# A graph layer on one core: source blocks of 732 instead of 640, overflow edges fetched inside the loop, and 128 edge ranges instead of 120

## The chip, the core and the metric

The kernel runs on one core of a Trainium2 chip. A core has TensorE (PE: matmuls, with PEld for its weight loads), VectorE (DVE), ScalarE (ACT), GpSimd (POOL), SyncE (SP, which here only issues transfers) and 16 DMA engines that all transfers share. Each engine runs its own list of instructions in order; they meet through semaphores. The metric is the device time of one execution in microseconds (us). Three runs of the kernel before took 16521.81, 16530.51 and 16532.21 us; the median is 16530.51.

## The reference

100,000 nodes have 64 features each. There are 3,300,000 edges (src, dst), sorted by dst: 1.6 million random pairs in both directions and one self-loop per node.

```
h = relu(layernorm(x))
y[e] = concat(h[dst], h[src] - h[dst]) @ W.T + b      for each edge e
s = segment_sum(y, dst);  cnt = segment_sum(1, dst)
out = x + where(cnt > 0, s / max(cnt, 1), 0)
```

The layer is linear in h[src], so what costs time is the sum of h[src] over the edges of each dst; the two products with W follow once per node.

## The kernel before, in words

**Table.** A first stage computes h and writes it to DRAM as `h3`: for each node 194 bf16 values, that is h cut into three bf16 parts (3 x 64), a one for the count and one value of padding, 388 bytes. Matmuls use the first 193 columns.

**Two ways to sum edges.** The edges are split by position. The last part goes through `chunks` (L344): 3584 edges at a time; POOL gathers the rows h3[src] with 28 indirect DMAs of 128 rows each (L388), DVE builds a one-hot matrix of dst (`one_hot`, L336 to L342), PE multiplies it with the rows, 28 matmuls of 193 columns (L393), and POOL adds the sums to `acc` in DRAM (L365 or L370). The first part is cut into `NW` = 120 *ranges* of 16,256 edges, which go through `pairs` (L743) two at a time (60 *sets*). Both ways share all engines, and the amounts of each are constants: `U0` sets and `PA` chunks come before a loop, and each of the loop's three iterations does `SB` sets and `KB` chunks.

**Sorting the ranges.** `sort_windows` (L415) sorts each range by source, one range per partition, all 120 at once: each merge step is a copy on ACT (L449) and a min and a max on DVE (L450, L451). It yields a nominal cost in ns after each step, and the main program then issues one chunk gather for every `GATHER` ns (1230) of it. At step 40 and at every second step after it, one block of `h3` is copied to `tables` in DRAM (L891, on SP); `tables` holds per partition what a block load needs in one run. Nothing ties these copies to the sort, so the scheduler that orders the instruction lists may move them forward.

**Slots.** A source block is `CS` = 640 nodes, in two halves of 320. In every sorted range, each half of a block gets `KS` = 64 slots. `fill_slots` (L681) fetches the keys of the slots by indirect DMA, 12 for each group of six blocks (L692), and DVE and ACT turn them into source numbers (`sr_d`) and dst numbers (`dt_d`). Edges of a half beyond its 64 slots, up to `SPILL` = 128 per range, are found by `find_beyond` (L634): 128 scans on DVE (L641), 120 indirect DMAs for their keys (L663), and two small tables `xs_d` and `xt_d` in DRAM.

**A set in `pairs`.** It steps through `NE` = 162 items: `NCB` = 157 blocks, four items of self-loops, and one item of overflow edges. `fetch` (8 items ahead) has SP load tables (three blocks per load, three buffers, L764), `srs` and `dt` (six blocks per load), the rows of the set's own nodes, and `xs` and `xt`; POOL gathers the overflow rows (L782). `one_hots` (two items per instruction) compares on DVE: `gh` picks a source within three sub-blocks of 128 (L796), `dh` places it among 512 dst nodes (L339). `pick` multiplies: three matmuls of 193 columns for each range and block (L822), then two copies on ACT (L825, L826). `put` adds into PSUM: eight matmuls for each item (L836). With halves of 320 nodes, sub-blocks 0 to 2 serve one half and 2 to 4 the other, so the middle one is shared and a `limit` test (L706, L707) keeps the halves apart.

The first `U0` = 3 sets start while `fill_slots` still runs: from its fourth group on, three steps (six items) of `pairs` follow each group. The remaining steps of these sets, with chunk gathers between, follow after it, then the rest of the `PA` = 71 chunks, then the loop.

Sizes that follow from the constants:

```
              sets  before loop / per iteration   chunks before / per iteration   items   blocks
before          60        3 / 19                        71 / 102                   162     157
after           64        1 / 21                        59 / 94                    144     137
```

Of the kernel before, what the change touches and what calls it, by code (L numbers as in the profile page):

```python
# [13 lines left out]
F32 = mybir.dt.float32  # L14
BF16 = mybir.dt.bfloat16
# [9 lines left out]
DVE = mybir.EngineType.DVE  # L25

# [4 lines left out]
SB = 19  # L31
KB = 102
U0 = 3
KG = 16
JH = 14
LAG = 3
GATHER = 1230
# [5 lines left out]
CS = 640  # L43
NB = CS // P
KH = P // 2
# [3 lines left out]
SPILL = 128  # L49
# [39 lines left out]
FIRST = 71  # L89
# [3 lines left out]
def gnn_preln(ctx: ExitStack, tc, x, src_w, dst_w, src_p, dst_p, src_a, dst_a, wT, b, out, V, E):  # L93
# [32 lines left out]
    NE = NS + 1  # L126
# [3 lines left out]
    RT = max(R, NCB * CS)  # L130
# [5 lines left out]
    assert NT == 4 and NB == 5 and CSH == 2 * P + KH  # L136
    assert 2 * C == P and NS % 2 == 1 and NW <= P and PA >= 0
# [13 lines left out]
    xs_d = dram.tile([SPILL, NW], I32, name="xs_d")  # L151
    xt_d = dram.tile([SPILL, NW, NH * D], I16, name="xt_d")
    tables = dram.tile([NTB, P, TG, NB * CT], BF16, name="tables")
# [157 lines left out]
    with tc.tile_pool(name="rows", bufs=5) as rows, \  # L311
# [103 lines left out]
        def sort_windows(keys, piece, small, ps):  # L415
# [32 lines left out]
            def exchange(lo, hi, tmp):  # L448
                nc.scalar.copy(tmp, lo)  # L449
                nc.vector.tensor_tensor(lo, tmp, hi, ALU.min)  # L450
                last[DVE] = nc.vector.tensor_tensor(hi, tmp, hi, ALU.max)  # L451
# [160 lines left out]
            nc.gpsimd.iota(first, pattern=[[CS, NS], [CSH - KH, 2]], base=BIAS >> 10, channel_multiplier=0)  # L612
            turned = piece.tile([NW, 2], F32, name="turned", bufs=1)
            nc.vector.tensor_scalar(turned, par, float(CSH - KH), None, op0=ALU.mult)
# [3 lines left out]
            limit = small.tile([NW, 2], F32, name="limit", bufs=1)  # L618
            nc.vector.tensor_scalar(limit[:, 0:1], par[:, 0:1], float(KH), float(CSH), op0=ALU.mult, op1=ALU.add)
            nc.vector.tensor_scalar(limit[:, 1:2], par[:, 0:1], float(-KH), float(CSH + KH), op0=ALU.mult, op1=ALU.add)  # L620
# [10 lines left out]
            slots[:] = at_i, first, row, fit, over, limit  # L631
            last.pop(DVE)

        def find_beyond(piece):  # L634

            row, fit, over = slots[2:5]
# [8 lines left out]
            nc.vector.tensor_scalar(xno, iota[:NW, :SPILL], over[:, NHB - 1:], None, op0=ALU.is_ge)  # L645
            nc.vector.tensor_add(xpos, xpos, iota[:NW, :SPILL])
# [5 lines left out]
            b_ps = g_ps.tile([P, 512], F32, name="gp")  # L652
            b_ps = b_ps[:, :2 * NW].rearrange("p (i w) -> p i w", i=2)
            for i in range(2):
                nc.tensor.transpose(b_ps[:, i], beyond[:, i], ident[:NW, :NW])
            xat = piece.tile([P, NW], I32, name="xat", bufs=1)
            nc.vector.tensor_copy(xat, b_ps[:, 0])
            xno = piece.tile([P, NW], F32, name="xno", bufs=1)
            nc.vector.tensor_copy(xno, b_ps[:, 1])
            yield  # L660
            kx = piece.tile([P, NW], I32, name="kx", bufs=1)
            for w in range(NW):
                last[POOL] = nc.gpsimd.indirect_dma_start(  # L663
                    out=kx[:, w:w + 1], out_offset=None, in_=ksort,
                    in_offset=bass.IndirectOffsetOnAxis(ap=xat[:, w:w + 1], axis=0))
                if w % 8 == 7:
                    yield
            xs = piece.tile([P, NW], I32, name="xs", bufs=1)
            nc.vector.tensor_scalar(xs, kx, 10, None, op0=ALU.logical_shift_right)
            nc.vector.tensor_scalar(xs, xs, float(-(BIAS >> 10)), float(V), op0=ALU.add, op1=ALU.min)  # L670
            nc.sync.dma_start(xs_d, xs)
            nc.vector.tensor_scalar(kx, kx, 1, CH - 1, op0=ALU.logical_shift_right, op1=ALU.bitwise_and)
            rx = piece.tile([P, NW], F32, name="rx", bufs=1)
            nc.vector.scalar_tensor_tensor(rx, xno, float(2 * CH), kx, op0=ALU.mult, op1=ALU.add)
            xt = piece.tile([P, NW, NH, D], I16, name="xt", bufs=1)
            for half in range(NH):
                nc.vector.tensor_scalar(xt[:, :, half], rx[:, :, None].to_broadcast([P, NW, D]), float(-half * HALF), None,
                                        op0=ALU.add)
            nc.sync.dma_start(xt_d.rearrange("s w i -> s (w i)"), xt.rearrange("s w h d -> s (w h d)"))

        def fill_slots(piece):  # L681
            at_i, first, limit = *slots[:2], slots[5]
# [3 lines left out]
            for c0 in range(0, NS, SL):  # L686
# [13 lines left out]

                df = piece.tile([NW, SL, P], F32, name="df", bufs=1)
                past = df.bitcast(I32).rearrange("w c (q s) -> w (c q) s", q=2)[:, :2 * mb]
                if mb:
                    for q in range(2):
                        of = [a.rearrange("w (c q) s -> w c q s", q=2)[:, :, q] for a in (past, sr[:, :2 * mb])]
                        nc.vector.tensor_scalar(*of, limit[:, q:q + 1], float(2 * CS), op0=ALU.is_ge, op1=ALU.mult)  # L706
                    nc.vector.tensor_tensor(sr[:, :2 * mb], sr[:, :2 * mb], past, ALU.add)  # L707
# [35 lines left out]
        def pairs(base, n, late=None):  # L743
# [4 lines left out]
            def fetch(t):  # L748
# [12 lines left out]
                if s < NCB and s % TG == 0:  # L761
                    m = min(TG, NCB - s)
                    tabs[u, s // TG] = tab = load.tile([P, TG, NB, CT], BF16, name="tab")
                    nc.sync.dma_start(tab[:, :m].rearrange("p c b f -> p (c b f)"),  # L764
                                      tables[s // TG][:, :m].rearrange("p c x -> p (c x)"))
# [5 lines left out]
                if s == (late if late and u == 0 else NE // 4):  # L771
                    at = ds((base + u) * 2, 2)
                    xs = load.tile([P, 2], I32, name="xs", bufs=2)
                    nc.sync.dma_start(xs, xs_d[:, at])
                    xt = load.tile([P, 2 * NH, D], I16, name="xt", bufs=2)
                    nc.sync.dma_start(xt.rearrange("p i d -> p (i d)"), xt_d[:, at].rearrange("s w i -> s (w i)"))
                    rows_x = load.tile([P, 2, CT], BF16, name="rows_x", bufs=2)
                    beyond[u] = xs, xt, rows_x
                if s == (NE - 2 if late and u == 0 else NE // 3):
                    xs, xt, rows_x = beyond[u]  # L780
                    for i in range(2):
                        last[POOL] = nc.gpsimd.indirect_dma_start(  # L782
                            out=rows_x[:, i], out_offset=None, in_=h3,
                            in_offset=bass.IndirectOffsetOnAxis(ap=xs[:, i:i + 1], axis=0))

            def one_hots(t):
                u, s = divmod(t, NE)
                if u < n:
                    m = min(2, NS - s)
# [3 lines left out]
                    for a, z, to in ((0, mb, NT - 1), (mb, m, NT)):  # L793
                        if a < z:
# [6 lines left out]
                    one_hot(dh[:, :m].rearrange("p c i (h n) -> p (c i h) n", h=NH),  # L801
                            dts[u, s // SL][:, c:c + m].rearrange("p c i d -> p (c i) d"), HALF)
                    if m < 2:
                        one_hot(dh[:, 1].rearrange("p i (h n) -> p (i h) n", h=NH), beyond[u][1], HALF)
# [248 lines left out]
```

## Time and profile before

| what | value |
|---|---|
| median of three runs | 16530.51 us |
| the profiled execution's own time | 16529.2 us |
| its span, first to last instruction | 16527.4 us |
| PE busy | 13495.8 us (82%) |
| DVE busy | 13631.9 us (82%) |
| POOL busy | 11625.4 us (70%) |
| ACT busy | 10590.2 us (64%) |
| DMA, mean over the span | 240 GB/s |
| loop, three iterations | about 3995 to 16203 us |

The page gives for each engine its busy time, then the span in 40 slices, where a digit is the busy share in tenths. PEclk is the granted TensorE clock, also in tenths. A group line names source line, engine, operation, output and inputs, then busy time, mean ns of one, and the idle time ahead of it with what ended it. "issue" marks idle time in which the engine waited for nothing that the profile shows. A busy share over the whole span mixes stages with different limits, so stages are read in windows of time.

### The profile page before, as it was taken

The page shows a single profiled execution, that of the slowest core. Times are in us where ns is not written, and L with a number is a line of the kernel's source. Part 1 is how long each engine was busy: PE and PEld are TensorE (multiplying, and loading weights), DVE is VectorE, ACT ScalarE, POOL GpSimd, SP SyncE. Part 2 cuts the span into 40 slices and gives each one's busy share as a digit, 9 for nine tenths or more (in the row PEclk, how much of TensorE's full clock was granted, in tenths as well). Part 3 has the DMA queues.
Part 4 walks back from the last instruction along what each step waited for, and adds up shares of the span by engine and source line. Part 5 has one row for each costly group of instructions (what it writes and reads, how often), then busy time and mean ns, then how long its engine had stood idle before and what let it go on. Part 6 is the DMA issues. An engine that isn't in the chain of part 4 may idle for free. (4 is left out here: it accounts for less than half of the span.)

```text
span 16527.4 us, 393944 instructions
## 1 busy us (share of the span) xinstructions
PE 13495.8 (82%) x149665; PEld 12959.6 (78%) x149665; DVE 13631.9 (82%) x14528; ACT 10590.2 (64%) x21095; POOL 11625.4 (70%) x11771
## 2 busy tenths in 40 slices
PE   6011110379999999999999999999999999999996
PEld 5011110369999999999899999999989999999996
DVE  6699996468888888888788888888878888888884
ACT  5144335466777777777677777777767777777772
POOL 4577777755777777777677777777767777777765
PEclk7555555689999999999999999999999999999998
DMA  8931112478999989999899999999879999999997
GB/s 295 152 50 39 39 39 63 139 221 255 279 281 280 279 279 279 281 279 278 253 280 279 280 279 279 278 281 278 278 249 279 281 282 280 279 280 279 279 276 282
DMA packets 1769028, 3974.67 MB, mean 240 GB/s; under 512 B 941660, under 2 KB 949607, under 8 KB 1759101
## 3 DMA queue, kind: packets, MB, share of 16 engines
q1 hardware_dynamic: 1289510, 3354.10, 61.8%
q0 software_dynamic: 473424, 569.44, 17.1%
q8 instruction: 1181, 19.35, 0.5%
q10 hardware_dynamic: 4176, 25.74, 0.4%
q14 instruction: 737, 6.04, 0.1%
HBM read 3750.40 MB, written 236.66 MB: 241 GB/s over the span
## 5 line engine op out<-in xcount | busy, mean ns | idle before, releaser
L388 POOL DMA_INDIRECT nb<-h,si x10556 | 10059.1, 953 | 3469.0 <-issue 3083.0
L836 PE MATMUL total<-gs,dh 128*128 128x193 bf16 x77280 | 8067.4, 247 | 65.2 <-ACT whole L844 29.1
L339 DVE TENSOR_TENSOR dh<-dt,c 128x2048 bf16<-128x2048 int16 x4860 | 5893.8, 1213 | 1718.9 <-PE total L836 1660.1
L836 PEld LDWEIGHTS <-dh 128*128 128x128 bf16 x77760 | 6725.8, 97 | 447.3 <-issue 85.1
L825 ACT CAST gs<-gp 64x386 bf16<-64x386 f32 x9420 | 4480.0, 476 | 3506.8 <-PE gp L822 3476.5
L822 PE MATMUL gp<-tab,gh 128*128 128x193 bf16 x56520 | 6356.8, 247 | 251.8 <-DVE gh L796 145.4
L822 PEld LDWEIGHTS <-gh 128*128 128x128 bf16 x58440 | 5092.8, 98 | 275.2 <-DVE gh L796 148.7
L796 DVE TENSOR_TENSOR gh<-srs,c 128x1536 bf16<-128x1536 int16 (+2 forms) x4920 | 4614.7, 939 | 29.1 <-PE gp L822 25.3
L826 ACT CAST gs<-gp 64x386 bf16<-64x386 f32 x9420 | 4494.5, 477 | 109.3
L393 PE MATMUL ps<-nb,hot 128*128 128x193 bf16 x10556 | 1805.6, 264 | 2131.1 <-DVE sums L405 1892.7
L393 PEld LDWEIGHTS <-hot 128*128 128x128 bf16 x10556 | 1044.7, 105 | 2196.3 <-DVE sums L405 1940.6
L449 ACT COPY tmp<-keys 120x1536 f32<-120x1536 f32 (+26 forms) x606 | 750.8, 1248 | 1352.5 <-DVE keys L451 1051.1
L450 DVE TENSOR_TENSOR keys<-tmp,keys 120x1536 f32<-120x1536 f32 (+26 forms) x606 | 867.3, 1466 | 71.2 <-ACT tmp L449 69.8
L451 DVE TENSOR_TENSOR keys<-tmp,keys 120x1536 f32<-120x1536 f32 (+26 forms) x606 | 869.0, 1464 | 1.3
L339 DVE TENSOR_TENSOR hot<-near,c 128x1792 bf16<-128x1792 int16 x754 | 814.2, 1080 | 0.1
L370 POOL DMA_DIRECT2D acc<-sums x306 | 305.9, 1000 | 287.4 <-DVE dh L339 102.4
L855 POOL DMA_DIRECT2D acc<-wsums x120 | 168.4, 1403 | 443.0 <-DVE wsums L851 150.5
L692 POOL DMA_INDIRECT kf<-ksort,at_i x322 | 330.3, 1026 | 110.2 <-issue 93.6
L697 DVE TENSOR_SCALAR sr<-kf 120x768 int32<-120x768 int32 (+1 forms) x27 | 15.3, 568 | 460.4 <-DMA kf<-ksort,at_i 443.5
L828 ACT CAST gs<-gp 128x386 bf16<-128x386 f32 x240 | 115.7, 482 | 203.2 <-PE gp L822 201.5
L1010 ACT COPY catT<-c_ps 128x512 f32<-128x512 f32 x112 | 56.2, 534 | 278.1 <-PE c_ps L1008 278.1
L726 PE MATMUL gp<-ident,df 120*128 120x120 f32 x161 | 30.5, 328 | 247.6 <-ACT df L718 222.5
(169 smaller groups left out, 4101.6 us busy)
## 6 DMA issues: line engine op xcount, KB each, us to landing
tab<-tables SPq DMA_DIRECT2D x3120, 727.5 KB
srs<-sr_d SPq DMA_DIRECT2D x1560, 384.0 KB
nb<-h,si POOLq DMA_INDIRECT x10556
tables<-h SPq DMA_DIRECT2D x157, 242.5 KB
h<-parts SPq DMA_DIRECT2D x28, 1358.0 KB
dt_d<-dt SPq DMA_DIRECT2D x26, 1440.0 KB
dt<-dt_d SPq DMA_DIRECT2D x1560, 24.0 KB
acc<-zeros SPq DMA_DIRECT2D x28, 910.0 KB
```

What stands on the lines that cost most here:

```text
L339: nc.vector.tensor_tensor(out.rearrange("p k (a d) -> p k a d", d=D), numbers[:, :, None].to_broadcast(shape), upto[:shape[0], :n].rearran ...
L388: last[POOL] = nc.gpsimd.indirect_dma_start(out=nb[:, j], out_offset=None, in_=h3, in_offset=bass.IndirectOffsetOnAxis(ap=si[:, u, j:j + 1 ...
L393: nc.tensor.matmul(ps, lhsT=before[1][:, j], rhs=before[2][:, j, :CE], start=j == 0, stop=j == J - 1)
L449: nc.scalar.copy(tmp, lo)
L450: nc.vector.tensor_tensor(lo, tmp, hi, ALU.min)
L451: last[DVE] = nc.vector.tensor_tensor(hi, tmp, hi, ALU.max)
L692: last[POOL] = nc.gpsimd.indirect_dma_start(out=kf[:, c, q], out_offset=None, in_=ksort, in_offset=bass.IndirectOffsetOnAxis(ap=at_i[:, c0 ...
L796: nc.vector.tensor_tensor(gh[:, a:z, :, :to].rearrange("p c i b s -> p (c i) b s"), srs[u, s // SL][:, c + a:c + z].rearrange("p c i s -> ...
L822: nc.tensor.matmul(gp[:, i], lhsT=ghots[t][:, i, b], rhs=of[:, :CE], start=b == 0, stop=b == len(parts) - 1)
L825: nc.scalar.copy(gs[t][:KS], gp[:KS])
L826: nc.scalar.copy(gs[t][KS:], gp[KS:, ::-1])
L836: nc.tensor.matmul(total[:, o, b % 2 * CE:b % 2 * CE + CE], lhsT=dhots[t][:, i, b * P:b * P + P], rhs=gs[t][:, i] if s < NS else beyond[u] ...
```

## The change

- Blocks have 732 sources, in halves of 366. Each half has three sub-blocks of its own: two of 128 rows and one of 110 (`KL`). A table load grows from 5 to 6 sub-blocks per block; the `limit` test is gone.
- There are 137 blocks, 141 items with slots, and three overflow items (`SPILL` = 384), 144 in all.
- `find_beyond` makes 384 scans and stores positions (`xat_d`) and flags (`xno_d`). Keys and rows of overflow edges are fetched in `fetch`, in every set: six gathers of keys, a few DVE instructions, six gathers of rows. Before, the keys were fetched once for all ranges and each set gathered two times for rows.
- The copies from `h3` to `tables` are issued by ACT, two per block, each tied behind the sort's last ACT copy.
- 128 ranges (64 sets), 59 chunks and one set before the loop, 94 chunks and 21 sets in an iteration. `GATHER` is 1250, and the index loads of `chunks` take 8 chunks at a time instead of 16.

```
-SB = 19
-KB = 102
-U0 = 3
-KG = 16
+SB = 21
+KB = 94
+U0 = 1
+KG = 8
-GATHER = 1230
+GATHER = 1250
-CS = 640
-NB = CS // P
-KH = P // 2
+CS = 732
+NB = 3
+KL = CS // 2 - (NB - 1) * P
-SPILL = 128
+NG = 3
+SPILL = NG * P
-FIRST = 71
+FIRST = 59
...
-    NE = NS + 1
+    NE = NS + NG
...
-    tables = dram.tile([NTB, P, TG, NB * CT], BF16, name="tables")
+    tables = dram.tile([NTB, P, TG, 2 * NB * CT], BF16, name="tables")
...
         def find_beyond(piece):
...
-            kx = piece.tile([P, NW], I32, name="kx", bufs=1)
-            for w in range(NW):
-                last[POOL] = nc.gpsimd.indirect_dma_start(
-                    out=kx[:, w:w + 1], out_offset=None, in_=ksort,
...
+            for i, (of, kind, to) in enumerate(((xpos, I32, xat_d), (xno, F32, xno_d))):
...
+                x = piece.tile([P, NW, NG], kind, name=f"x{i}", bufs=1)
+                nc.vector.tensor_copy(x, b_ps.rearrange("p g w -> p w g"))
+                nc.sync.dma_start(to, x)
...
-                past = df.bitcast(I32).rearrange("w c (q s) -> w (c q) s", q=2)[:, :2 * mb]
-                if mb:
-                    for q in range(2):
...
-                        nc.vector.tensor_scalar(*of, limit[:, q:q + 1], float(2 * CS), op0=ALU.is_ge, op1=ALU.mult)
-                    nc.vector.tensor_tensor(sr[:, :2 * mb], sr[:, :2 * mb], past, ALU.add)
...
-                if s == (late if late and u == 0 else NE // 4):
+                if s == (late if late and u == 0 else NE // 2):
                     at = ds((base + u) * 2, 2)
...
+                    xat = load.tile([P, 2, NG], I32, name="xat", bufs=2)
+                    nc.sync.dma_start(xat, xat_d[:, at])
+                    xno = load.tile([P, 2, NG], F32, name="xno", bufs=2)
+                    nc.sync.dma_start(xno, xno_d[:, at])
...
+                if s == (late + 4 if late and u == 0 else NE * 5 // 8):
+                    xat, xno, kx = beyond[u]
                     for i in range(2):
+                        for g in range(NG):
+                            last[POOL] = nc.gpsimd.indirect_dma_start(
+                                out=kx[:, i, g:g + 1], out_offset=None, in_=ksort,
...
+                if s == (late + 6 if late and u == 0 else NE * 6 // 8):
...
+                    nc.vector.tensor_scalar(xs, kx, 10, None, op0=ALU.logical_shift_right)
+                    nc.vector.tensor_scalar(xs, xs, float(-(BIAS >> 10)), float(V), op0=ALU.add, op1=ALU.min)
+                    nc.vector.tensor_scalar(kx, kx, 1, CH - 1, op0=ALU.logical_shift_right, op1=ALU.bitwise_and)
+                    nc.vector.scalar_tensor_tensor(xno, xno, float(2 * CH), kx, op0=ALU.mult, op1=ALU.add)
...
+                    for half in range(NH):
+                        for i in range(2):
+                            nc.vector.tensor_scalar(xt[:, :, i, half], ...
...
+                    for g in range(NG):
+                        for i in range(2):
+                            last[POOL] = nc.gpsimd.indirect_dma_start(
+                                out=rows_x[:, g, i], out_offset=None, in_=h3,
...
-                            parts = [(b, row[:, b + 2 * i]) for b in range(NT - 1)]
+                            parts = [(b, row[:, NB * i + b]) for b in range(NB)]
                         for b, of in parts:
-                            nc.tensor.matmul(gp[:, i], lhsT=ghots[t][:, i, b], rhs=of[:, :CE],
+                            k = KL if block and b == NB - 1 else P
+                            nc.tensor.matmul(gp[:, i], lhsT=ghots[t][:k, i, b], rhs=of[:k, :CE],
...
-                        nc.sync.dma_start(tables[k // TG, :, k % TG].rearrange("p (b f) -> p b f", b=NB),
-                                          h3[k * CS:(k + 1) * CS].rearrange("(b p) f -> p b f", b=NB))
+                        with tc.issue_after(last[ACT].ins):
+                            for half in range(2):
+                                at = k * CS + half * CSH
+                                nc.scalar.dma_start(
+                                    tables[k // TG, :, k % TG].rearrange("p (i b f) -> p i b f", i=2, b=NB)[:, half],
+                                    h3[at:at + NB * P].rearrange("(b p) f -> p b f", b=NB))
...
-                    steps = pairs(0, U0, NE - AHEAD // 2)
+                    steps = pairs(0, U0, NE - AHEAD)
```

## The prediction

> **What bounds the kernel now.** I read the slices first, then windows of time by stage, then the waits of each stage, then single gathers. The page's slices show a front of about 4000 us in which PE is nearly idle, and a loop in which it is full:
>
> ```profile
> PE   6011110379999999999999999999999999999996
> DVE  6699996468888888888788888888878888888884
> POOL 4577777755777777777677777777767777777765
> DMA  8931112478999989999899999999879999999997
> ```
>
> Windows cut at the stages (us; busy time and count of PE, PEld, DVE, ACT, POOL; granted clock, DMA share, GB/s): slot filling, rest of the front, three loop iterations, last stage.
>
> ```profile
> 2905.00:3512.00 607.00, 252.26 (x1941) 225.15 (x1942) 290.69 (x553) 280.48 (x581) 456.44 (x447) 0.66 0.49 153
> 3512.00:3995.00 483.00, 472.51 (x5359) 455.54 (x5358) 402.13 (x435) 347.17 (x730) 217.75 (x219) 0.99 0.87 264
> 3995.00:8063.00 4068.00, 4014.80 (x46000) 3882.81 (x45997) 3482.22 (x3745) 2908.39 (x6122) 2910.79 (x3036) 1.00 0.89 276
> 8063.00:12133.00 4070.00, 4013.99 (x45986) 3881.58 (x45986) 3480.41 (x3735) 2906.74 (x6118) 2908.68 (x3034) 1.00 0.90 276
> 12133.00:16203.00 4070.00, 4014.64 (x45986) 3882.39 (x45986) 3480.36 (x3736) 2906.77 (x6118) 2910.73 (x3034) 0.99 0.90 276
> 16203.00:16527.00 324.00, 200.13 (x1176) 181.56 (x1176) 136.84 (x227) 56.17 (x112) 200.67 (x56) 0.80 0.83 319
> ```
>
> An iteration is PE's: 4014 of 4070 us busy, 45,986 matmuls at 87.3 ns each; the other 56 us are its start and end. The remaining 483 us of the front are PE's too. Slot filling is POOL's: its gathers run back to back, and DVE waits for their data. The chain of waits (waiting engine and line, releaser, us in total, times, longest) in the loop, 6000 to 8000 us:
>
> ```profile
> POOL nb L388 <- issue: 413.0, 1356, 0.3
> DVE dh L339 <- PE total L836: 261.9, 523, 1.3
> PE gp L822 <- DMA tab<-tables: 1.0, 2, 0.7
> ```
>
> and from the sort's start to the first slot fetch, 440 to 2910 us:
>
> ```profile
> POOL nb L388 <- issue: 498.7, 1636, 0.6
> DVE own L437 <- DMA s<-in_src_w: 85.4, 10, 38.6
> POOL nb L388 <- DMA nb<-h,si: 79.6, 147, 4.2
> ```
>
> POOL's "issue" gap is 0.30 us after each gather of 0.95: a gather costs 1.249 us from start to start. So POOL looks 70% busy but is full wherever this gap is its only idle time. The timeline shows where the front hangs on it: DVE ends the sort at 2741, POOL is still at gathers and begins the first slot fetch only at 2910.7:
>
> ```profile
> 2909.49 0.94 POOL L388 DMA_INDIRECT nb<-h,si  x1 [0.30 <-issue]
> 2910.74 0.99 POOL L692 DMA_INDIRECT kf<-ksort,at_i  x1 [0.31 <-issue]
> ```
>
> **What the Trainium skill says.** "TensorE: Matmul & The Clock Gate", section LDWEIGHTS: loading weights costs by columns, not by contraction rows. The trace agrees: loads of 96 rows (L301) have a median of 100 ns, those of 128 rows in the loop a mean of 97. So sub-blocks of 110 rows are costed like full ones. "DMA: Bandwidth & Descriptors", section "Issuing engines are not separate DMA queues": transfers from SP, ACT and POOL run on the same 16 engines. The trace agrees: packets of 7168 bytes have a median of 272 ns from SP's queue and from ACT's. So moving the table copies to ACT moves only issue time and their date. "HBM Reference", Specifications: a core streaming alone reaches about 425 GB/s. Here the last stage reached 400 GB/s in a 25 us window (16250 to 16275).
>
> **The change, part by part.**
>
> *Loop, PE.* Matmuls per set before: 157 blocks x 6 + 4 x 8 + 162 x 8 = 2270. After: 137 x 6 + 4 x 8 + 144 x 8 = 2006. An iteration had 19 x 2270 + 102 x 28 = 45,986, as the window shows; it gets 21 x 2006 + 94 x 28 = 44,758. At 87.3 ns that is 3907, with the 56 us of start and end 3963. Three iterations: 11,889 against 12,210 (3995 to 16,205), -321.
>
> *Loop, what must stay hidden.* POOL: 94 x 28 + 21 x 12 = 2884 gathers against 2894, x 1.249 = 3602; 94 additions of about 1.3 and 42 of about 1.75 make 196; 3798 in all, of 3963. DVE per set: 71 `dh` x 1.219 + 1.4, about 68 `gh` x 0.947 + 3, eight small new instructions (0.15 each, like L405's 148 ns, so 1.2), `wsums` 3.3: 160 us x 21 + 94 x 2.7 = 3614; the same count for before gives 3680, so DVE stays as hidden as it was. ACT falls with the blocks. If POOL's cover went, each us over 3963 would show.
>
> *Loop, new waits.* In a set POOL waits for `xat` before the key gathers, DVE for the keys before `xs`, POOL for `xs` before the row gathers. Behind DVE's wait are queued the one-hots, and PE waits for these. The steps lie 18 items apart, about 22 us of PE time; six gathers and the landing need about 10. POOL waiting for DVE gives up only its lead: rows of a chunk are used a chunk (28 gathers, 35 us) later. I take 0; the upper end is one 2.5 us step per set, 50 us per iteration.
>
> *Loop, DMA.* Table bytes per set: 157 blocks x 128 x 1940 = 39.0 MB become 137 x 128 x 2328 = 40.8; `srs` 10.5 becomes 9.2. With chunk rows an iteration moved 276 GB/s x 4070 us = 1123 MB; it gets 21 x 51.0 + 94 x 1.39 + 12 (overflow rows, additions, the rest) = 1214, which in 3907 us is 311 GB/s. Can the engines give that? The share of 0.90 suggests not (0.90 x 311/276 = 1.01), but it counts slowed packets: table packets of 5820 bytes have a median of 222 ns and a mean of 261. When buffers refill after an iteration's start the same mix ran at 332 GB/s (12,180 to 12,200). A table load lands a median of 5.7 us after its issue (99%: 7.2), and it is issued two loads, 7.9 us, ahead of its use; PE waited for tables 1.0 us in 2000. Loads grow by a fifth, so the margin nearly goes. Lower end 0, upper end the rate of 300 GB/s (below). I take 1% of stalls: 35 us per iteration, +105.
>
> *Up to the slots.* Before, 64 of 71 chunks were gathered ahead of the first slot fetch: 490 (first gather) + 1792 x 1.249 + 58 additions x 1.93 = 2840; the other 71 us are waits and slowed gathers, most in 490 to 860, when the table copies run as a burst. After, all 59 chunks: 490 + 2063 + 102 = 2655, to 2726 if these 71 us stay. DVE: 2741, less 20 counts of 1.03, less 85 us of waiting for `s` behind the burst, plus 0 to 80 for ACT: 274 issues x 0.33 to 0.55 us (ACT's `hb` issues; the shortest of SP's table copies) are 90 to 150 us of ACT, hidden because ACT needs 1.25 and DVE 2.9 us in a full step. Slots start at 2690 (2640 to 2740) instead of 2911: -220.
>
> *Slot filling.* Before 601 us, 442 gathers. After 282: 24 groups x 15.4 = 370 us by POOL. DVE per group: 16 scans (0.48 + 0.08 with 314 columns, now 274) about 7.4, three steps 6.3, slot work 2.5, so 16.2; groups with scans and steps took 22 before. I take 18.8 x 24 = 450 (375 to 530): -150.
>
> *Rest of the front.* Before, 171 steps of `pairs`, 483 us. After, 9 steps, but they need the first overflow edges: store, load, six key gathers, six row gathers, four transfers, about 35 us, then the last additions: 60 us (40 to 120). -423.
>
> *Loads on SP*: `xat` and `xno` replace `xs` and `xt` one for one; index loads come twice as often at half the size, 70 us ahead of use; SP waits for free buffers most of the time. 0. The slots suffice: counted on the inputs, a range has at most 334 overflow edges of 384.
>
> Sum against the span: 16,527 - 321 + 105 - 220 - 150 - 423 = 15,518; the median lies 3 us above the span: **15,520**.
>
> **Rivals.** *A: DMA bounds the loop.* For it: the 0.90 share, and table loads already in flight nearly all the time. At 300 GB/s, 1214 MB need 4047 + 56 = 4103 per iteration; 16,527 - 793 (front) + 3 x 33 = 15,835. *B: POOL and DVE hold each other up at the new waits.* POOL has 4% left. If each set loses 8 us, as the waits for `wsums` cost POOL at a set's end today (8.4 us at 6009), 63 x 8 = 504, in place of the 105 for DMA 15,920. Against it: the 22 us distance. *C: slower.* The loop must lose 264 us per iteration to eat the front's 793, that is 4334: a feed under 1214/4278 = 284 GB/s. At today's 276: 4455 x 3 gives 16,890. Against it: 332 GB/s and PE's 1.0 us of waiting; at 276 PE set the pace, not DMA. *D: the copies tied to the sort, or the order the scheduler finds, cost the front its gain*: slots at 2911, filling 600: 15,890.
>
> **How the numbers follow.** As forecast 0.62, its own range 15,330 to 15,690; A 0.19; B 0.07; C 0.04; D 0.05; better than 15,330 0.03. All low ends together (2640 + 375 + 40 + 11,889 + 324) give 15,270; all high ends, with A's loop, 2740 + 530 + 120 + 12,309 + 324 = 16,020. Range 15,300 to 16,000. Within 0.2% (33 us, about what this measurement can tell from no change): 0.01; faster 0.95, slower 0.04.
>
> **What would show it.** An iteration window with 44,758 matmuls, near 4000 us, 305 GB/s or more; over 4080 with PE waiting for `tab` is A; PE or DVE waiting for `kx` or `xs` is B. First slot fetch near 2690, loop start near 3200, no burst at 500 to 860. The prediction is wrong if the loop's GB/s stays near 280, or if the loop starts after 3400.

## The result and the profile after

The changed kernel takes 18,030.95 us (median of 4 runs, 18,016.28 to 18,034.72) where the kernel before takes 16,530.94: a ratio of 1.0906, 95% interval 1.0889 to 1.0923. It is slower by 1,500 us; the forecast was 15,520 (range 15,300 to 16,000), faster by about 1,010. The profiled execution spans 18,027.3 us.

The slices of the changed kernel, for PE, DVE, POOL and DMA, each digit tenths of a slice of 451 us:

```profile
PE   5111114688888788887788888888688888788886
DVE  5889997677777666776677777676577777677775
POOL 4777776555666665546666665666566655666654
DMA  7344125688888777877778888777678888788887
```

The front is shorter, as forecast: PE starts to fill in slice 7 (2,704 to 3,155 us), and the loop begins in slice 8. But where the loop had nines for PE it has mostly eights, and POOL, DVE and DMA are less busy too. All four have time to spare, so the engines wait for each other.

Windows of the changed kernel cut at its stages, in the order of columns used before: slot filling with the rest of the front, the three iterations, the last stage.

```profile
2751.00:3271.00 520.00, 274.53 (x2168) 245.53 (x2168) 364.40 (x1043) 290.39 (x588) 299.69 (x295) 0.70 0.64 202
3271.00:8074.00 4803.00, 3966.74 (x44776) 3832.75 (x44776) 3401.15 (x3838) 2812.59 (x5922) 2899.89 (x3021) 0.91 0.80 255
8074.00:12878.00 4804.00, 3961.70 (x44763) 3827.21 (x44762) 3400.39 (x3837) 2812.62 (x5922) 2896.93 (x3021) 0.91 0.80 256
12878.00:17688.00 4810.00, 3967.18 (x44755) 3830.60 (x44753) 3400.56 (x3834) 2812.61 (x5922) 2896.43 (x3020) 0.91 0.80 255
17705.00:18027.00 322.00, 200.53 (x1176) 181.84 (x1176) 135.81 (x227) 56.22 (x112) 200.81 (x56) 0.80 0.83 321
```

An iteration has about the forecast number of matmuls (44,758), but lasts 4,803 us and not 4,000; of these PE is busy 3,967. DMA moves 255 GB/s, less than the 276 before; that it could move more is shown by e4 below (308). Five of the waits of the same 2,000 us of the loop that the prediction showed, 6000 to 8000 (waiting engine and line, what it waits for, us in total, times, longest):

```profile
DVE xs L764 <- DMA kx<-ksort,xat: 366.9, 9, 82.3
PE total L835 <- DVE dh L341: 319.4, 6, 78.1
POOL nb L390 <- issue: 311.7, 1023, 0.3
DVE dh L341 <- PE total L835: 200.0, 394, 1.6
POOL acc L372 <- DVE sums L407: 125.8, 6, 39.8
```

The first line is new: DVE waits for the keys of the overflow edges, 9 times about 41 us, and behind it PE waits for DVE's one-hots. Over the whole run it is 2,572.9 us in 64 sets. The timeline shows one such wait (start, duration, engine and line, idle time before it and its releaser). DVE's side, and PE's first matmul after it:

```profile
11339.30 0.94 DVE L791 TENSOR_TENSOR gh<-srs,c 128x1536 bf16<-128x1536 int16 x1
11422.54 0.17 DVE L764 TENSOR_SCALAR xs<-kx 128x6 int32<-128x6 int32 x1 [82.30 <-DMA kx<-ksort,xat]
...
11424.17 1.47 PE L835 MATMUL total<-gs,dh 128*128 128x193 bf16 x8 [77.98 <-DVE dh L341]
```

POOL's side of the same time:

```profile
11235.56 0.88 POOL L372 DMA_DIRECT2D acc<-sums  x1 [39.80 <-DVE sums L407]
11265.12 1.06 POOL L390 DMA_INDIRECT nb<-h,si  x1 [28.68 <-DMA si<-in_src_p]
...
11411.79 0.94 POOL L390 DMA_INDIRECT nb<-h,si  x1 [0.31 <-issue]
11413.03 0.94 POOL L758 DMA_INDIRECT kx<-ksort,xat  x1 [0.30 <-DMA nb<-h,si]
11414.28 0.94 POOL L758 DMA_INDIRECT kx<-ksort,xat  x1 [0.30 <-issue]
```

The six key gathers and their landing take 9.5 us (11,413.03 to 11,422.54), about the 10 of the prediction. They were not slow; they began late. While DVE stood still, POOL issued chunk gathers (and one addition) back to back for 73 us (11,340 to 11,413), and came to the keys only then. Not long before, POOL itself had stood idle for 40 us waiting for sums that DVE makes and for 29 us waiting for a list of indices.

Why the keys stand there is seen in the instruction lists of the compiled programs. The kernel's text writes the keys (item 90 of a set), then 18 items with about 16 chunk gathers, then xs (item 108). The lists that the scheduler made of it differ. The beginning of the loop's body in POOL's list of the changed kernel, with counts (the trace runs them in this order):

```
nb<-h,si x140
kx<-ksort,xat x6
nb<-h,si x4
acc<-sums
nb<-h,si
rows_x<-h,xs x6
```

So 140 chunk gathers lie ahead of the first set's keys, where DVE's list puts xs behind steps to which 58 of them belong (2,632 gathers spread evenly over an iteration's steps). With the keys' own six, the keys stand 88 gathers, 110 us of POOL's time at 1.249 each, behind the point where DVE's list needs them. Over the 21 sets of an iteration it is 43 to 100 gathers, on average 80; "80 gathers late" is said of this below, and "early" where the keys stand ahead of that point. So POOL must lead, that is be further along its own list than PE and DVE are along theirs, by that much or DVE waits.

The Trainium skill, "PSUM — Partial Sum Buffer", section "Engine vs sequencer instructions", says that the queues of ScalarE, VectorE and GpSimdE are strictly first in, first out. The trace agrees: in those 82.3 us DVE ran nothing, although the next one-hot of its list, for which PE was waiting, started as soon as the three small instructions were through (11,422.90 us).

### The profile page after: what moved, and what is told of

Same layout as the page of the kernel before. It is cut to its first block, busy times and chain, and to the rows that moved or that the text cites. A ratio compares the mean times of both kernels' runs of the same rounds, so it can differ in the third digit from the quotient of the medians.

```text
span 18027.3 us, 372080 instructions
## 1 busy us (share of the span) xinstructions
PE 12896.2 (72%) x140825; PEld 12364.1 (69%) x140825; DVE 13037.0 (72%) x14805; ACT 9948.2 (55%) x19740; POOL 11079.4 (61%) x11223
## 5 line engine op out<-in xcount | busy, mean ns | idle before, releaser
L390 POOL DMA_INDIRECT nb<-h,si x9548 | 9102.1, 953 | 3894.7 <-issue 2815.7
L835 PE MATMUL total<-gs,dh 128*128 128x193 bf16 x72192 | 7634.8, 249 | 2043.5 <-DVE dh L341 2009.1
L824 ACT CAST gs<-gp 64x386 bf16<-64x386 f32 x8768 | 4169.7, 476 | 5771.9 <-PE gp L821 5751.0
L341 DVE TENSOR_TENSOR dh<-dt,c 128x2048 bf16<-128x2048 int16 x4544 | 5499.0, 1210 | 1385.0 <-PE total L835 1348.3
L821 PE MATMUL gp<-tab,gh 128*128 128x193 bf16 (+1 forms) x52608 | 6003.4, 249 | 202.1 <-ACT dt L703 109.1
L821 PEld LDWEIGHTS <-gh 128*128 128x128 bf16 (+1 forms) x54656 | 4826.9, 99 | 257.2 <-issue 121.1
L791 DVE TENSOR_TENSOR gh<-srs,c 128x1536 bf16<-128x1536 int16 x4608 | 4311.0, 937 | 40.6 <-PE gp L821 23.3
L825 ACT CAST gs<-gp 64x386 bf16<-64x386 f32 x8768 | 4183.6, 477 | 101.7
L764 DVE TENSOR_SCALAR xs<-kx 128x6 int32<-128x6 int32 x64 | 12.3, 192 | 2572.9 <-DMA kx<-ksort,xat 2572.9
L451 ACT COPY tmp<-keys 128x1536 f32<-128x1536 f32 (+26 forms) x606 | 750.3, 1248 | 1382.4 <-DVE keys L453 919.7
L372 POOL DMA_DIRECT2D acc<-sums x282 | 280.5, 995 | 1226.7 <-DVE sums L407 1014.2
L452 DVE TENSOR_TENSOR keys<-tmp,keys 128x1536 f32<-128x1536 f32 (+26 forms) x606 | 867.0, 1466 | 225.7 <-ACT tmp L451 224.2
L453 DVE TENSOR_TENSOR keys<-tmp,keys 128x1536 f32<-128x1536 f32 (+26 forms) x606 | 867.8, 1463 | 1.4
L758 POOL DMA_INDIRECT kx<-ksort,xat x384 | 365.4, 951 | 407.6 <-DMA xat<-xat_d 294.5
```

The lines of the kernel that those rows point to most:

```text
L341: nc.vector.tensor_tensor(out.rearrange("p k (a d) -> p k a d", d=D), numbers[:, :, None].to_broadcast(shape), upto[:shape[0], :n].rearran ...
L390: last[POOL] = nc.gpsimd.indirect_dma_start(out=nb[:, j], out_offset=None, in_=h3, in_offset=bass.IndirectOffsetOnAxis(ap=si[:, u, j:j + 1 ...
L451: last[ACT] = nc.scalar.copy(tmp, lo)
L758: last[POOL] = nc.gpsimd.indirect_dma_start(out=kx[:, i, g:g + 1], out_offset=None, in_=ksort, in_offset=bass.IndirectOffsetOnAxis(ap=xat[ ...
L791: nc.vector.tensor_tensor(gh[:, a:z, :, :to].rearrange("p c i b s -> p (c i) b s"), srs[u, s // SL][:, c + a:c + z].rearrange("p c i s -> ...
L821: nc.tensor.matmul(gp[:, i], lhsT=ghots[t][:k, i, b], rhs=of[:k, :CE], start=b == 0, stop=b == len(parts) - 1)
```

## The experiments

The theories. **1**: DVE's wait for kx is the whole loss; in form **1a** because 18 items are too little as written, in form **1b** because of where the two lists put keys and xs. **2**: with the wait gone, DMA bounds the loop (15,800 to 16,000). **3**: POOL is full, and the wait only shows it.

In e1 to e4 the kernel before ran at 16,525 us, in e5 to e8 at 16,531, in e9 and e10 at 16,592, in e13 and e14 at 16,537. e4 and e8 to e13 give medians of four executions; e1, e2, e3, e5, e6, e7 and e14 are one execution each, and what is read from them is hundreds of us.

**e1: xs without the keys.** A first try at taking DVE's dependence away.

```diff
-  nc.vector.tensor_scalar(xs, kx, 10, None, op0=ALU.logical_shift_right)
+  nc.vector.tensor_scalar(xs, kc, 0, None, op0=ALU.logical_shift_right)   # kc: a fixed tile
```

> The six key gathers of a set are still issued, but xs and xno are computed from a constant tile, so DVE no longer waits for keys and the overflow edges' rows and columns are not the true ones; everything else is as in the changed kernel. Theory 1 (the loop loses its time to DVE's wait for kx, and to nothing else): 15,400 to 15,700 us, the 2573 us of DVE waiting for kx gone and no other wait above 300 us in its place. Theory 2 (DMA takes over once the wait is gone): 15,800 to 16,000, with PE waiting for tab more than 200 us. Theory 3 (POOL is full, the wait only shows it): over 17,000, POOL waiting little and PE or DVE waiting for nb or rows_x.

Measured: 17,994 us, outside theories 1 and 2 and in the range of theory 3. The waits of e1, one line:

```profile
DVE xs L766 <- DMA rows_x<-h,xs: 2497.6, 45, 78.4
```

The wait for kx is gone, and the same instruction now waits as long for something else: xs has two buffers, and writing the next has to wait until POOL's row gathers have read the one of two sets before. Freed of the keys, xs moved forward in DVE's list, until it was tied to POOL's list by its buffer. So it isn't the keys as such. A wait for rows_x is also what theory 3 named, but with POOL waiting little, and in e1's loop POOL's waits other than the issue gap add up to 3,024 us. This run alone doesn't decide; e4 and e7 do.

**e2: the keys written 78 items earlier.**

```diff
-  if s == (late if late and u == 0 else NE // 2):          # xat
+  if s == (late if late and u == 0 else 2):
-  if s == (late + 4 if late and u == 0 else NE * 5 // 8):  # kx
+  if s == (late + 4 if late and u == 0 else 12):
```

> Only the places of emission differ: xat is fetched at item 2 instead of 72 and the keys at item 12 instead of 90, xs stays at item 108, so 96 items (about 118 us) instead of 18 lie between keys and xs as they are written. Theory 1a (the distance as written is too short): 15,400 to 15,800. Theory 1b (the order in which the scheduler puts them into the two lists decides: read off the lists, DVE's xs has moved forward with the keys, and in POOL's list the keys stand 54 to 102 chunk gathers, mean 84, behind the point where DVE's list needs them, as against 43 to 100 in the changed kernel): 17,500 to 18,300, with DVE waiting for kx over 2000 us in all.

Measured: 17,987 us, and the waits of e2 say

```profile
DVE xs L764 <- DMA kx<-ksort,xat: 2461.5, 62, 86.7
```

Form 1a falls: 96 items between keys and xs as written, and DVE waits as before. Form 1b had it. The keys stand 83 gathers late in the lists (54 to 102, and 11 in the first set of an iteration): the scheduler moved xs forward with them.

**e3: chunk gathers held behind the keys.** In POOL's list only. What is written under `issue_after(x)` may not be put ahead of x in its list.

```diff
+  if late is None:                              # in the loop
+      pin[0] = last[POOL].ins                   # the last key gather of a set
...
+  with tc.issue_after(pin[0]) if pin[0] else nullcontext():
       last[POOL] = nc.gpsimd.indirect_dma_start(out=nb[:, j], ...)
```

> Chunk gathers written after a set's key gathers may not be put ahead of them in POOL's list; distances and work as in the changed kernel. In the lists the keys then stand 25 gathers behind the point where DVE's list needs them instead of 80, and the row gathers 34 gathers ahead of PE's need. Theory 1b: POOL has to lead by 31 gathers and a landing, some 42 us, where the additions let it lead by 52 or more: DVE's wait for kx falls below 500 us and the time to 15,500 to 16,000. Theory 1a (18 items are too few in themselves): over 17,000. Theory 2: 15,800 to 16,100 with PE waiting for tab. Theory 3: over 17,000.

Measured: 16,131 us; the waits of e3:

```profile
DVE xs L768 <- DMA kx<-ksort,xat: 608.2, 61, 19.4
```

The order of the list alone, no work and no distance changed, gives back 1,900 us. Time and wait lie 131 and 108 us above the ranges of 1b: leading by 31 gathers isn't free.

**e4: the order written out.** Keys at item 12, xs at 60, row gathers at 108; chunk gathers held behind keys and row gathers, xs behind the one-hot written before it.

```diff
+  if s == (late + 6 if late and u == 0 else 60):
+      with tc.issue_after(pin[1]) if late is None else nullcontext():
+          nc.vector.tensor_scalar(xs, kx, 10, None, op0=ALU.logical_shift_right)
...
+  if s == (late + 6 if late and u == 0 else 108):
       rows_x = load.tile(...)                   # and the six row gathers
+      if late is None: pin[0] = last[POOL].ins
```

> All the work of the changed kernel, the keys at item 12, xs at item 60, the row gathers at item 108, with chunk gathers held behind the keys and the row gathers, and xs held behind the one-hot written before it. In the lists the keys then stand 36 gathers ahead of DVE's need and the row gathers 34 ahead of PE's. Theory 1 in either form: 15,400 to 15,700 us, ratio to before 0.93 to 0.95, DVE's wait for kx under 50 us. Theory 2: 15,800 to 16,000 with PE waiting for tab more than 200 us. Theory 3: over 17,000.

Measured: 15,573 us (15,572.75 to 15,586.68), ratio 0.9424, interval 0.9408 to 0.9440. It beats both kernels, with all the work of the change. Its three iterations:

```profile
3274.00:7247.00 3973.00, 3918.25 (x44776) 3792.09 (x44776) 3402.78 (x3839) 2807.62 (x5922) 2901.73 (x3021) 1.00 0.95 308
7247.00:11234.00 3987.00, 3917.96 (x44760) 3792.11 (x44758) 3402.78 (x3836) 2807.66 (x5922) 2898.65 (x3020) 0.99 0.95 308
11234.00:15241.00 4007.00, 3920.48 (x44764) 3792.33 (x44762) 3403.16 (x3837) 2807.67 (x5922) 2897.43 (x3021) 0.99 0.94 307
```

PE is full again, at 308 GB/s. Two of its waits, over the whole run:

```profile
DVE xs L769 <- DMA kx<-ksort,xat: 9.0, 1, 9.0
PE gp L831 <- DMA tab<-tables: 80.0, 93, 9.2
```

DVE's wait for kx is gone. PE waits little for tab, so theory 2 falls. POOL had the time: theory 3 falls too. Nor do slower matmuls explain the loss, although the granted clock was 0.91 in the changed kernel's loop and is 0.99 to 1.00 here: for the same matmuls PE is busy 3,965 us an iteration there and 3,919 here, and an iteration is 816 us longer there. In the loop POOL's waits other than the issue gap add up to 659 us here and to 2,995 in the changed kernel, where it was late for the keys and idle besides.

**e5: one part of the change alone, on the kernel before.** Old blocks, old slots; the keys, now 2 gathers a set, go into the loop.

```diff
-  kx = piece.tile([P, NW], I32, name="kx", bufs=1)     # all keys, in the slot filling
-  for w in range(NW): ... indirect_dma_start(out=kx[:, w:w + 1], ...)
+  if s == (late + 4 if late and u == 0 else NE * 5 // 8):
+      for i in range(2): ... indirect_dma_start(out=kx[:, i:i + 1], ...)
+  if s == (late + 6 if late and u == 0 else NE * 6 // 8):
+      nc.vector.tensor_scalar(xs, kx, 10, None, op0=ALU.logical_shift_right)   # and on to rows_x
```

> The kernel before (blocks of 640, 128 overflow slots, 157 blocks, three sets ahead of the loop, table copies as before) with one part of the change alone: the keys of the overflow edges are gathered in the loop, 2 gathers at item NE*5//8, xs at NE*6//8, as the changed kernel does it, instead of 128 gathers in the slot filling. In the lists the two keys stand 77 to 97 chunk gathers, mean 88, behind the point where DVE's list needs them. Theory 1b: DVE waits for kx 30 to 45 us in each of 57 sets, 1700 to 2550 us, less up to 160 us that the front saves: 18,000 to 19,000. If the larger blocks or the fuller DMA make the loss (theories 2 and 3): 16,300 to 16,700.

Measured: 18,274 us, 1,743 above the kernel before. The waits of e5:

```profile
DVE xs L770 <- DMA kx<-ksort,xat: 1761.8, 52, 85.0
POOL acc L370 <- DVE sums L405: 885.7, 38, 38.2
```

So this part alone, on the old blocks, makes a loss of this size, with the same wait. e4 is the other half of the argument: the new blocks and 308 GB/s without the loss.

**e6: additions two chunks later.** In the changed kernel POOL also waits for DVE's sums, 40 us at a time (L372). A mutual hold was suspected: POOL can't come to the keys because it waits for sums, which DVE, waiting for the keys, can't make.

```diff
-LAG = 3
+LAG = 5
```

> The changed kernel with one constant changed: an addition is put in POOL's list 4 chunks behind its gathers instead of 2, with two more buffers for the sums. In the lists the addition then stands a median of 110 gathers behind the point where DVE makes its sums instead of 83, so POOL may lead DVE by that much before it must wait for it; the keys stand where they did, 43 to 100 gathers (mean 80) late. If the loss is a mutual hold (POOL can't reach the keys because it waits for sums that DVE, waiting for the keys, can't make): DVE's wait for kx falls by more than half, 15,700 to 16,900. If POOL simply hasn't the time to get ahead, the lead it may have doesn't matter: 17,700 to 18,100.

Measured: 17,971 us, DVE's wait for kx 2,528. The suspicion in this form falls. The time is in the range of the alternative, but its reason, that POOL hasn't the time, doesn't hold: POOL stood idle. Its longest waits in e6's loop, 3300 to 17,590:

```profile
POOL nb L390 <- PE gp L821: 879.9, 57, 74.8
POOL kx L758 <- DMA xat<-xat_d: 592.2, 12, 68.8
POOL nb L390 <- DMA si<-in_src_p: 412.2, 9, 74.3
POOL nb L390 <- PE total L835: 406.0, 24, 75.6
```

The wait for sums fell from 974 us to 144, and others took its place: for chunk buffers that PE frees, for xat and for indices that come by SP. By their lines these gates (what has to happen before POOL may go on) move at PE's pace; that is read from the lines and was not tried. POOL's waits in the loop add up to 3,035 us, about as many as in the changed kernel. Which of these gates would have to be opened together for POOL to keep a lead of 80 gathers stays open.

**e7: no xs at all.** The clean form of e1: the row gathers take the fixed tile.

```diff
-  nc.vector.tensor_scalar(xs, kx, 10, ...)      # and the two that follow
+  xs = kc
```

> As e1, but DVE no longer writes xs at all: the row gathers take one fixed tile of indices, so nothing on DVE depends on POOL's key or row gathers; only xno and xt are still computed, and the overflow edges' rows and columns are not the true ones. The lists put the row gathers about 140 gathers ahead of PE's need. If the loss of e1 was the wait of xs for the last reader of its buffer, which stands as late in POOL's list as the keys: 15,400 to 15,750. If a list with early keys and rows is slow in itself, or POOL is full: over 16,500.

Measured: 15,638 us. The lists are not held here, and in POOL's list the key gathers stand among the chunk gathers exactly where they stand in the changed kernel, so their place by itself costs little (the run is 65 us above e4). What costs is that DVE depends on it.

**e8: the row copies on SP, not tied to the sort.** e4 with this part of the change undone.

```diff
-  with tc.issue_after(last[ACT].ins):
-      nc.scalar.dma_start(tables[...], h3[...])
+  nc.sync.dma_start(tables[...], h3[...])
```

> As e4, with one part of the change undone: the row copies are issued by SP and not tied to the sort, as before. The burst of copies at the sort's start comes back, and ACT is rid of 274 issues. If tying the copies to the sort brings what the prediction took (71 us of POOL's and 85 us of DVE's waits behind the burst, of which the first slot fetch gets 70): first slot fetch at 2800 to 2840 instead of 2752, 15,630 to 15,680. If the waits behind ACT's copies cost as much as the burst did: 15,560 to 15,590. If the copies on ACT cost more than the burst: 15,450 to 15,540.

Measured: 15,560 us, ratio 0.9416, interval 0.9400 to 0.9432, no different from e4: the middle forecast, at its low end. The first slot fetch is at 2,719 us, 33 earlier than in e4. DVE's waits from 440 to 2760 us, the changed kernel first:

```profile
DVE keys L452 <- ACT tmp L451: 224.2, 81, 78.4
```

and e8:

```profile
DVE own L441 <- DMA s<-in_src_w: 75.4, 9, 33.7
DVE keys L454 <- ACT tmp L453: 69.0, 78, 2.4
```

Tied to ACT, the copies take away the wait for s (75 us) and 46 us of other waits for transfers, but DVE then waits 155 us more for ACT, up to 78 us at a time.

**e9: 18 items, held.** The changed kernel's places (72, 90, 108; the row gathers at 124), with both lists held.

```diff
-  if s == (late + 6 if late and u == 0 else 108):   # e4's place of the row gathers
+  if s == (late + 6 if late and u == 0 else 124):
```

> The places of the changed kernel (xat at item 72, keys at 90, xs at 108, 18 items apart; the row gathers alone moved on to item 124) with both lists held to them as in e4. In the lists the keys then stand 9 gathers (some 14 us of PE's pace) ahead of DVE's need, and the row gathers 20 ahead of PE's. If the prediction's sum for these waits was right (18 items are enough for six gathers and a landing) and only the lists did not keep it: 15,540 to 15,650, DVE's wait for kx under 130 us in all (2 us a set). If 18 items are too few even when kept: DVE waits for kx over 400 us, 15,900 or more.

Measured: 15,856 us where the kernel before took 16,592; ratio 0.9562, interval 0.9546 to 0.9578. DVE's wait for kx:

```profile
DVE xs L769 <- DMA kx<-ksort,xat: 254.5, 36, 12.3
```

Neither range holds it. With its order kept, the written distance costs 4 us a set.

**e10 to e13: one pass of 63 sets.** On e8, to save two starts and ends of an iteration.

```diff
-SB = 21
-KB = 94
+SB = 63
+KB = 282
```

> As e8, with the loop of three iterations of 21 sets and 94 chunks made one iteration of 63 sets and 282 chunks. An iteration of e8 lasts 3981 to 3989 us, of which 44,758 matmuls at 87.3 ns are 3907: 74 to 82 us go to its start and end, and two of the three are saved. Theory 1 with PE as the bound: 15,400 to 15,450. If a body three times as long costs as much (its instructions fetched, or an order found worse by the scheduler): 15,540 or more.

Measured: 19,489 us, ratio 1.1746 (1.1726 to 1.1766), a miss: far into the open range of 15,540 or more. In e10's waits PE lacks tables, and SP's queue, which loads them, has a new wait (PE for the whole run, SP for 6000 to 10,000 us):

```profile
PE gp L831 <- DMA tab<-tables: 3847.1, 149, 76.7
```

```profile
SPq L751 <- DMA kx<-ksort,xat: 828.7, 40, 74.5
```

In the longer body the scheduler moved the loads of xat forward in SP's list by up to three sets. There SP stands until POOL's key gathers have read the buffer, with the table loads behind it. e11 holds xat and xno behind the table load written before them:

```diff
+  with tc.issue_after(pin[2]) if late is None else nullcontext():
       nc.sync.dma_start(xat, xat_d[:, at])
```

> As e10, with one more list held: on SP, xat and xno are held behind the table load written before them. In SP's list of e10 they stand up to 150 table loads, three sets, ahead of their place (in e8 46 apart, one set), and there SP waits for the keys two sets earlier to release xat's buffer while the tables behind it are late. If that is what made e10 slow: the table loads run as in e8, PE waits for tab under 300 us in all, and with two starts and ends of an iteration saved 15,400 to 15,460 where the kernel before has 16,530 (ratio 0.931 to 0.936). If the long body is slow in itself: over 17,000.

> The kernel of e11 once more, since there the kernel before itself took 27,046 us, so that e11's times say nothing of the loop. Expected as for e11: if the misplaced loads of xat on SP made e10 slow, the table loads run as in e8, PE waits for tab under 300 us in all, 15,400 to 15,460 where the kernel before has 16,530 (ratio 0.931 to 0.936). If the long body is slow in itself: over 17,000.

e11 and e12 ran where the kernel before itself took 27,046 and 27,066 us, so their 26,237 and 26,265 can't be set beside the other runs.

> The kernel of e11 and e12 once more, since both fell where the kernel before took 27,046 and 27,066 us. Expected as for e11: if the misplaced loads of xat on SP made e10 slow, PE waits for tab under 300 us in all, 15,400 to 15,460 where the kernel before has 16,530 (ratio 0.931 to 0.936). If the long body is slow in itself: over 17,000.

Measured in e13: 16,900 us, ratio 1.0223 (1.0206 to 1.0240), between the two forecasts. PE's waits for tables fell from 3,847 us to 1,417, and SP's from the loads of xat to another. The waits of e13, PE's of the whole run, then SP's from 3300 to 15,400:

```profile
PE gp L833 <- DMA tab<-tables: 1417.0, 85, 70.4
```

```profile
SPq L354 <- DMA nb<-h,si: 1425.0, 90, 73.0
```

Now the loads of chunk indices stand in front of the tables, waiting for gathers to free their buffer. That holding xat takes away some 2,520 us is shown (the difference of the two ratios, of 16,537); that the rest is the same thing with si is read from this line and was not tried.

**e14: only xs held.** DVE's list alone moved.

```diff
+  with tc.issue_after(pin[1]) if late is None else nullcontext():
       nc.vector.tensor_scalar(xs, kx, 10, None, op0=ALU.logical_shift_right)
```

> The changed kernel with DVE's list alone held: xs behind the one-hot written before it, POOL's list as it was. In the lists the keys then stand 9 to 68 gathers, mean 46, behind DVE's need (80 in the changed kernel, 25 in e3), but the row gathers 3 to 66 gathers behind PE's need, where they were 11 behind on average before. Theory 1b: DVE's wait for kx between that of e3 (10 us a set) and that of the changed kernel (40), about 20 us a set, 1000 to 1700 us in all, part of the gain lost to PE waiting for rows_x: 16,600 to 17,600 where the kernel before has 16,530. If holding DVE's list were enough by itself: under 16,000.

Measured: 16,507 us, beside 16,537 for the kernel before. That is 93 us under the range of 1b, and DVE waits 502 us where at least 1,000 were expected. The waits of e14:

```profile
DVE xs L766 <- DMA kx<-ksort,xat: 502.1, 25, 43.9
PE total L837 <- DMA rows_x<-h,xs: 385.3, 148, 17.8
```

The stall was split: part stays with DVE, part went to PE, which now lacks the rows, since these stand as late in POOL's list as they did and xs comes later.

**The experiments together.** What each kernel loses against e4, which has the same work, beside DVE's wait for kx (e9 scaled by 16,525 / 16,592):

| kernel | keys in the lists, against DVE's need | DVE waits for kx, us | us above e4 |
|---|---|---|---|
| changed | 80 gathers late | 2,573 | 2,458 |
| e2 | 83 late | 2,461 | 2,414 |
| e14 | 47 late | 502, and PE for rows_x 385 | 934 |
| e3 | 25 late | 608 | 558 |
| e9 | 9 early | 254 | 219 |
| e4 | 36 early | 9 | 0 |

In each row the wait accounts for the loss to within 120 us. It falls with the lateness, not in proportion: in e14, 47 late cost DVE less than 25 late in e3, and PE paid the other part.

## Why the prediction was wrong

The step that failed is "Loop, new waits", taken as 0 with an upper end of 50 us per iteration. It measured 2,573 us over the run, about 40 a set and 844 an iteration. The other terms can be checked in e4, which does all of the changed kernel's work without this wait; the front in the changed kernel itself gives the same numbers to within 4 us.

| step | forecast, us | measured in e4, us |
|---|---|---|
| first slot fetch | 2,690 | 2,752 |
| slots and rest of the front | 450 + 60 = 510 | 522 |
| loop, three iterations | 11,889 + 105 = 11,994 | 11,967 |
| last stage | 324 | 344 |
| span | 15,518 | 15,585 |

- **Loop, new waits: wrong.** Two sentences of it held: six gathers and their landing take about 10 us (9.5), and 18 items are about 22 us. The conclusion took the written order for the order of the lists, where the distance was -80 gathers. With the written order kept (e9) the step costs 4 us a set, above its upper end of 2.5; the 22 us were a little too few even so. Why is not shown; presumably POOL isn't at PE's pace at every moment. "POOL waiting for DVE gives up only its lead" missed what the lead is for: the keys stand 80 gathers deep in it.
- The trace of before could have warned. Its only chain of this kind, the row gathers, is written at item 54 of 162 and fetched 8 items ahead. That would be 116/162 of a set of 214 us, or 153 us, before the set's end. In the loop of the trace the gathers start 85 to 139 us before PE uses them there, about 118 on average: they stood late in POOL's list there too, 64 chunk gathers on average. Over two thirds of a set of distance, and no DVE instruction waiting for them, hid it.
- **Loop, PE and DMA: right.** 44,758 matmuls, and an iteration of 3,989 us in e4 against 3,998. The rate asked for was 311 GB/s, and 308 was given. The share of 0.90 in the trace before wasn't a ceiling: it stands at 0.95 here.
- **Up to the slots: the size was off by 62 us.** POOL's part was right: its last gather starts at 2,669, within the 2,655 to 2,726 forecast. But DVE ends the sort later than taken, since the copies on ACT hold up the sort's ACT step; with the copies back on SP (e8) the first slot fetch comes 33 us earlier, at 2,719. The changed kernel's timeline, the counterpart of the two lines shown of before:

```profile
2733.70 1.57 POOL L367 DMA_INDIRECT acc<-sums,to  x1 [33.32 <-DVE sums L407]
2751.39 1.28 POOL L673 DMA_INDIRECT kf<-ksort,at_i  x1 [16.12 <-DVE worst L898]
```

Before, DVE was done and POOL late; now POOL is idle 33 and 16 us and DVE is late. "0 to 80 for ACT" counted the issues' time; DVE's waits for ACT's step came to 155 us more than without the copies. What ACT waits for at the longest of them is not settled.

- **Slot filling and rest of the front: right** in sum (522 against 510).
- **Rivals.** B named the place, the two engines and the sign (DVE waiting for `kx`), but gave it 8 us a set, the price of another wait, and 7 in 100; 40 were measured. Its price was the mistake: what may stand ahead of the awaited instruction in the other list says how long an in-order engine can be kept waiting, here five chunk buffers of 28 gathers (140 gathers, 175 us), and not one step. The longest wait was 87 us. C, the rival on the slow side, was a DMA rate; the loop ran at 255 GB/s because it waited, not the other way round.

## What to carry to other kernels

When a change makes one in-order engine wait for another inside a scheduled loop, work the distance out from the compiled lists of both engines (or hold the order by hand); here the distance in the source said little, and moving the source apart (e2) moved both ends. In a list that work running ahead into its buffers keeps full, the urgent instructions can end up behind that work, so they have to be held in place, and what waits for them given room on its own list too. When such a wait is taken away, look at what the same instruction waits for next (e1), and who waits in its place (e14).

## What the runs showed of the hardware that had not been expected

- DMA: 308 GB/s through iterations of 4,000 us at a share of 0.95, with 80 us of PE waiting for tables in the whole run, after 276 GB/s at 0.90 in the kernel before.
- In e11 and e12 the kernel before took 27,046 and 27,066 us instead of 16,530. In e11's trace PE's weight loads show 8,736 us of idle time for which the profile has no releaser, up to 44 us at a time. The granted clock of the kernel before is 0.75 there, and 0.90 in the other runs. The cause is open.
